# Places for gathered rows lent by tables and weights, and a longer count, in a graph-network kernel

## The chip, the cores and the metric

The kernel runs on one core of one Trainium2 chip. The metric is the device time of one execution in microseconds (us), and the time of a kernel is the median over its runs. The engines are PE (TensorE, matmul; its loading of weights is shown apart as PEld), DVE (VectorE), ACT (ScalarE), POOL (GpSimd) and SP (SyncE, which issues DMAs).

## What is computed

A graph layer over N = 12,500 nodes of D = 256 features and M = 212,500 edges (src, dst), which come sorted by dst, followed by a mixture of 64 experts with the best two per node, a normalization over the nodes, and a layer normalization with a residual:

```python
deg_out = jnp.clip(jax.ops.segment_sum(ones, src, num_segments=n), 1.0)
deg_in = jnp.clip(jax.ops.segment_sum(ones, dst, num_segments=n), 1.0)
h = feats * jax.lax.rsqrt(deg_out)[:, None]
m = jax.ops.segment_sum(h[src], dst, num_segments=n) * jax.lax.rsqrt(deg_in)[:, None]
gc = m @ W_gc + b_gc
x = gc + (feats @ W_res + b_res)
y = x + _moe_ff(x, Wg, bg, w1, b1, w2, b2)      # top 2 of E = 64 experts, H = 512
y = (y - mean(y, 0)) * rsqrt(var(y, 0) + eps) * gamma + beta
return _layernorm(feats + y)
```

The change touches the first third: the gathering of h[src], its sums by dst, and the counting of deg_out.

## The kernel before, in words

**Rows.** The edges are cut into rows of 128. There are 1,593 of them, and a count CA = 480 of them makes the first phase. For a row c, Pool issues one indirect DMA that gathers 128 lines of 1 KB (128 KB) by `src_col[:, c]` into a place of 128 x 256 numbers in SBUF. DVE makes a one-hot matrix from the row's dst (`one_hot`, L881 to L895), 12 rows ahead (`AHEAD`); there are 5 tiles of four. PE multiplies one-hot by place into a PSUM bank (L924); in the trace one row is two matmul records. Twelve rows make a group (GR): then ACT copies the bank (`out_of`, L959), PE turns the sums (`turn`, L974), and DVE adds them to the nodes' sums in `acc` (`to_nodes`, L997). All of this is written out in order by `go` (L1691 to L1707): each row's gather, its matmul, the one-hot of the row 12 behind it, and then all other work whose row number has come (`at_row`, `later`, a heap of row numbers). So every engine has one fixed order, and a step is placed by a row number.

**What a row reads.** Rows below NE = 104 gather from the input x itself, since the scaled features h do not exist yet; the factor of each edge's source goes into the one-hot (`look` L606 on PE and `found` L614 on DVE look it up). Meanwhile x is loaded into `xs` (a part of `acc`), scaled by ACT and DVE (`scaled`, L625 and L627) and written by SP to h_d in DRAM (`h_out`, L631). Rows from 104 on gather from h_d.

**Where a row waits.** Rows 0 to 39 (EA) go to parts of `xs` that are still free, rows 40 to 47 to eight pieces of a table (`flat`, in the tile `tables`); both are issued ahead of the loop (`first_row` L461, `wait_at` L456). From row 48 (ES) on, rows go to a ring of RINGS x RR = 5 x 4 = 20 places. The first gather of each four waits for the last matmul of the four that had the places before (`row_last`, by `sync`).

**What else SP brings.** Around row 22 `zero_piece` (L670) copies zeros into two pieces of `acc` that the groups' sums are added to, and again at row 104 into four more. `lines_in` at row 92 clears a tail of two tables on DVE (L661) and loads lines of dst and src. `src_in` at row 98 loads src once more for counting, `weights_in` at row 106 loads the tables of weights (`wcat`, `bias`, and so on) that the phase behind row 480 needs.

**Counting.** deg_out has to be compared with what the kernel assumed. 68 groups (KG) of 25 columns of src are split into digits (`digits`), turned into one-hots by DVE (`compare`, `compare_b`, both through `hot`, L248) and ACT (Sign, L1590), and counted by PE in two PSUM banks (`tally`, L1595 and L1599). The numbers that DVE compares with, `lane_p`, lie in the upper part of the first of these banks. The groups stand evenly between the rows COUNT_FROM = 112 and COUNT_TO = 426. Five steps behind them (`counted` to `counted_e`, at COUNT_TO + 12 + 3 i) end in `bad_n`, a single number (L1627), which every engine reads behind row 480 to choose a branch (L1715). Beside counting, DVE marks (rows 108 to 158) and squeezes (rows 160 to about 353) the repeated edges, and lays them out in new columns behind that.

**Behind row 480.** The other rows go on in the same way, now with the node part of the layer in between, then the experts follow, and the normalizations.

Of the kernel before, what the change touches and what calls it, by code (L numbers as in the profile page):

```python
# [8 lines left out]
F32 = mybir.dt.float32  # L9
F16 = mybir.dt.float16  # L10
BF16 = mybir.dt.bfloat16
# [10 lines left out]
D = 256  # L22
# [10 lines left out]
EP = 125  # L33
EC = M // EP
# [12 lines left out]
HC = HG * GR  # L47
# [12 lines left out]
CA = PA * GR  # L60
# [5 lines left out]

NE = 104
EA = 40
ES = 48
ET = 56  # L70
NOWHERE = 2 * NP
BEHIND = (1 << 14) - 1
# [78 lines left out]
def gnn_moe_kernel(  # L151
# [18 lines left out]
    V, S, T, GP = nc.vector, nc.scalar, nc.tensor, nc.gpsimd  # L170
# [38 lines left out]
    slot_a = route.tile([P, NSLOT], I32)  # L209
# [9 lines left out]
    flat = tables.rearrange("p a b c -> p (a b c)")  # L219
# [10 lines left out]
    bias = edge.tile([P, DL], F32)  # L230
# [194 lines left out]
    def x_in(t0, n):  # L425
        r = rows(t0)
        nc.sync.dma_start(xs[:r, t0 : t0 + n], part_of(x, t0, n))
# [25 lines left out]
    place = place[:, :EC]  # L453


    def wait_at(c):  # L456
        if c < EA:
            return xs[:, ET + c]
        return flat.bitcast(F32)[:, (c - EA) * D : (c - EA + 1) * D]

    def first_row(c):  # L461
        GP.indirect_dma_start(
            out=wait_at(c),
            out_offset=None,
            in_=x,
            in_offset=bass.IndirectOffsetOnAxis(ap=src_col[:, c : c + 1], axis=0),
        )
# [52 lines left out]

    for v in range(OH):
        compare_lo(v)
    for c in range(EA, ES):
        first_row(c)
    V.tensor_copy(top_i, top8)
    V.tensor_scalar(
# [105 lines left out]


    def check_order():
        junk = flat.bitcast(BF16)[:EP, : EC - 1]
        V.tensor_tensor(junk, dst_t[:, 1:], dst_t[:, : EC - 1], op=ALU.is_lt)
        V.tensor_scalar(
            junk, junk, 0.5, None, op0=ALU.is_gt, op1=ALU.add, accum_out=bad[:EP, 6:7]
        )
# [9 lines left out]
        )  # L649

    def check_windows():
        junk = flat.bitcast(F32)[:, :HC]
        for k, (lim_of, op) in enumerate(((0.0, ALU.is_lt), (float(W), ALU.is_ge))):
            V.tensor_scalar(
                junk, rel[:, :HC], lim_of, None,
                op0=op, op1=ALU.add, accum_out=bad[:, k : k + 1],
            )

    def lines_in():
        V.tensor_mul(root, d_in, r_in)  # L660
        V.memset(l_dst[:, LAST:], BEHIND)  # L661
        V.memset(l_src[:, LAST:], 0)
        for t, e in ((l_dst, dst), (l_src, src)):
            nc.sync.dma_start(
                t[: NL - 1], e[HE : HE + (NL - 1) * L].rearrange("(p c) -> p c", c=L)
            )
            nc.sync.dma_start(t[NL - 1 :, :LAST], e[M - LAST :].rearrange("(p c) -> p c", p=1))
# [169 lines left out]
    def at_row(c, f):  # L837
        heapq.heappush(todo, (c, len(given_at), f))
        given_at.append(c)
# [16 lines left out]
    def sync(i, on):  # L856
        tc.add_manual_dep(
            i.ins, on.ins.name,
            mybir.DependencyInfo(mybir.DependencyClass.Sync, mybir.DependencyReason.DATA),
            reason="one wait for several",  # L860
        )
# [36 lines left out]
    def row(c):  # L898
        g, j = divmod(c, GR)
        last = j == GR - 1 or c == ROWS - 1  # L900
        u, k = divmod(c, RR)
        if c < ES:
            h_row = wait_at(c)
        else:
            r = ring[u % RINGS]
            h_row = r[:, k]
            i = GP.indirect_dma_start(  # L907
                out=r[:, k, :D],
                out_offset=None,
                in_=x if c < NE else h_d,  # L910
                in_offset=bass.IndirectOffsetOnAxis(ap=src_col[:, c : c + 1], axis=0),
            )
            if k == 0 and u - RINGS in row_last:
                sync(i, row_last.pop(u - RINGS))
        n = D
        if g >= HG:
            n = D1
            if k == 0:
                S.copy(r[:, :, D], mark[:, c - HC : c - HC + RR])
        if j == 0:  # L920
            p_of[g] = p_banks[g % 2][:, :D1]
            own(g)
        v, m = divmod(c, OR)
        i = T.matmul(  # L924
            p_of[g][:, :n], o_of[v][:, m], h_row[:, :n], start=j == 0, stop=last
        )
        if m == 0:
            sync(i, o_last.pop(v))
        if m == OR - 1:
            del o_of[v]  # L930
        if k == RR - 1 and c >= ES:
            row_last[u] = i
        if last:
            later(c, lambda t: out_of(g, n, t), 0.5)

# [708 lines left out]
        at_row(5 * i + 2, lambda t, a=t0 + n - BY_DVE: scaled(a, BY_DVE, False))  # L1644
        at_row(5 * i + 5, lambda t, t0=t0, n=n: h_out(t0, n))
    for i, (t0, n) in enumerate(second):
        at_row(min(t0 + n - ET, ES) + 1, lambda t, t0=t0, n=n: x_in(t0, n))
        a = 28 + 9 * i
        for k in range(n):
            at_row(a + k, lambda t, a=t0 + k: scaled(a, 1, True))  # L1650
        at_row(a + n, lambda t, t0=t0, n=n: h_out(t0, n))
# [4 lines left out]
        at_row(max(0, 4 * u - 35), lambda t, u=u: compare_lo(u))  # L1656
    for i in (0, NPW // 2):
        at_row(22, lambda t, i=i: zero_piece(i))
    for i, f in enumerate((check_order, check_runs, check_windows)):
        at_row(60 + 10 * i, lambda t, f=f: f())  # L1660
    at_row(92, lambda t: lines_in())
    at_row(98, lambda t: src_in())
    for i in (1, NPW // 2 + 1, 2, NPW // 2 + 2):
        at_row(104, lambda t, i=i: zero_piece(i))
    at_row(106, lambda t: weights_in())
    at_row(NE, lambda t: lanes())
    COUNT_FROM, COUNT_TO = 112, CA - 54
    for k in range(KG):
        c = COUNT_FROM + (COUNT_TO - COUNT_FROM) * k // KG
        if k % CK == 0:  # L1670
# [604 lines left out]
```

## Time and profile before

| | |
|---|---|
| three runs | 2998.6, 2994.85, 2983.08 us; median 2994.85 us |
| the profiled execution | 3004.58 us, of which its span is 3002.8 us |
| mean granted clock of PE | 0.94 |
| busy, share of the span | PE 82%, PEld 62%, DVE 55%, ACT 26%, POOL 68% |
| DMA | 563.72 MB, mean 188 GB/s |

All times below are in microseconds from the start of the span unless said otherwise. A line of a timeline gives the start, the duration, the engine, the source line, the operation, what is written from what is read, the count, and in brackets how long the engine was idle before it and what ended that. A line "A <- B: t, n, m" of the waits says that A waited t us in all for B, in n places, the longest m us. A line of windows gives the stretch, its length, then busy time and instructions for each engine that is asked for, the granted clock, the share of the DMA engines and GB/s. L followed by a number is a line of the kernel.

### The profile page before, as it was taken

The numbers are of one execution on the slowest core, as the hardware profiler recorded it, in microseconds if no ns is written. First come the engines' busy times: TensorE is split into PE (matmuls) and PEld (weight loads), VectorE is DVE, ScalarE is ACT, GpSimd is POOL, SyncE is SP. The second block draws the span as 40 slices with busy tenths as digits, with TensorE's granted clock in tenths as the row PEclk, the third lists the DMA queues.
The fourth block names the chain that finished last, engine by engine and source line by source line (L and its number), as shares of the span: only waits on it lengthen the run. The fifth ranks groups of instructions, "written<-read, shape, count | busy, mean of one in ns | idle before, by whom it ended". The sixth has DMA issues, their size and how long they took to land. (4 is left out here: it accounts for less than half of the span.)

```text
span 3002.8 us, 43600 instructions
## 1 busy us (share of the span) xinstructions
PE 2469.6 (82%) x13517; PEld 1865.1 (62%) x13517; DVE 1664.2 (55%) x6230; ACT 783.7 (26%) x2250; POOL 2048.3 (68%) x2145
## 2 busy tenths in 40 slices
PE   4756666777888777798999998999995799899895
PEld 4634445545655444576777777666773577777795
DVE  8868887644788634465344433343454544444247
ACT  2723444421111000122222222222221122222346
POOL 7677777677777777777777777777772767775200
PEclk9988989998999998999999999999997899999998
DMA  6953333336555444556666676676884567777868
GB/s 208 351 182 98 101 98 100 97 111 216 174 148 143 135 124 123 167 172 184 180 192 197 200 209 203 203 227 204 258 240 135 169 211 234 256 245 245 279 204 283
DMA packets 287463, 563.72 MB, mean 188 GB/s; under 512 B 56518, under 2 KB 194294, under 8 KB 279030
## 3 DMA queue, kind: packets, MB, share of 16 engines
q0 software_dynamic: 99120, 268.99, 30.9%
q1 hardware_dynamic: 174310, 278.75, 29.2%
q10 hardware_dynamic: 13792, 13.10, 1.4%
q8 instruction: 110, 1.80, 0.2%
q14 instruction: 131, 1.07, 0.1%
HBM read 494.32 MB, written 66.34 MB: 187 GB/s over the span
## 5 line engine op out<-in xcount | busy, mean ns | idle before, releaser
L907 POOL DMA_INDIRECT ring<-h_d,src_col x1489 | 1461.3, 981 | 469.3 <-issue 400.5
L924 PE MATMUL p<-ring,o 128*128 128x257 f32 (+1 forms) x3090 | 994.1, 422 | 217.2 <-DMA ring<-h_d,src_col 151.4
L924 PEld LDWEIGHTS p<-ring,o 128*128 128x128 f32 x3090 | 538.0, 202 | 410.2 <-DMA ring<-h_d,src_col 208.0
L894 DVE TENSOR_SCALAR o<-lane,rel 128x128 f32<-128x128 f32 x1489 | 380.2, 298 | 271.8 <-PE p L924 270.8
L1419 ACT ACTIVATE acc<-p,acc 128x128 f32<-128x128 f32 (+8 forms) x360 | 137.3, 381 | 742.6 <-PE p L1408 424.9
L1443 DVE TENSOR_TENSOR acc<-yp_a,acc 128x256 f32<-128x256 f32 (+7 forms) x127 | 53.2, 419 | 431.1 <-PE yp_a L1436 431.1
L1408 PE MATMUL p<-acc 128*128 128x128 f32 (+8 forms) x1440 | 248.5, 295 | 8.0 <-ACT s L959 2.1
L1408 PEld LDWEIGHTS p<-acc 128*128 128x128 f32 x1440 | 220.5, 191 | 53.7 <-ACT acc L1419 33.8
L1436 PE MATMUL yp_a<-acc 128*128 128x256 f32 (+7 forms) x1016 | 250.4, 391 | 0.0
L1922 PE MATMUL yp<-w,h 128*128 128x256 f32 (+7 forms) x1032 | 239.6, 382 | 7.3 <-DVE yo L1927 7.3
L1895 PE MATMUL hp<-xT,w 128*128 128x112 f32 (+17 forms) x1056 | 214.5, 358 | 31.2 <-DVE xT L1886 29.2
L248 DVE TENSOR_TENSOR acc<-bank,acc 125x2450 bf16<-125x2450 bf16 (+1 forms) x136 | 185.1, 1361 | 87.7 <-PE bank L1595 74.7
L1590 ACT ACTIVATE acc<-lane_b,acc 125x128 bf16<-125x128 bf16 x544 | 168.5, 389 | 232.8 <-PE bank L1599 226.0
L1895 PEld LDWEIGHTS hp<-xT,w 128*128 128x128 f32 x1056 | 178.1, 203 | 64.3 <-DVE xT L1886 33.4
L1595 PE MATMUL bank<-acc 125*128 125x98 bf16 x1156 | 104.3, 219 | 133.4 <-DVE acc L248 116.0
L1899 ACT ACTIVATE h<-hp,w 128x128 f32<-128x128 f32 (+16 forms) x264 | 113.0, 430 | 376.3 <-PE hp L1895 345.8
L1595 PEld LDWEIGHTS <-acc 125*128 125x128 bf16 x1156 | 84.7, 104 | 201.3 <-issue 158.0
L1922 PEld LDWEIGHTS yp<-w,h 128*128 128x128 f32 (+7 forms) x1032 | 167.9, 170 | 56.5 <-DVE yo L1927 10.2
L1436 PEld LDWEIGHTS yp_a<-acc 128*128 128x128 f32 (+7 forms) x1016 | 171.5, 174 | 48.4 <-issue 5.8
L1933 POOL DMA_INDIRECT z_d<-yo,tables x129 | 125.1, 970 | 92.1 <-DVE gate L1909 41.0
L1867 POOL DMA_INDIRECT xg<-xb_d,tables x129 | 125.3, 971 | 51.4 <-PE xtp L1882 18.5
L1372 POOL DMA_INDIRECT acc<-xa_d,tables x127 | 123.4, 972 | 42.8 <-issue 31.4
(375 smaller groups left out, 3481.8 us busy)
## 6 DMA issues: line engine op xcount, KB each, us to landing
w<-in_wpack SPq DMA_DIRECT2D x64, 1026.0 KB
acc<-in_wpack SPq DMA_DIRECT2D x128, 512.0 KB
ring<-h_d,src_col POOLq DMA_INDIRECT x1489
tables<-h_d SPq DMA_DIRECT2D x99, 128.0 KB
acc<-acc_d SPq DMA_DIRECT2D x14, 896.0 KB
xt<-in_x ACTq DMA_DIRECT2D x48, 256.0 KB
zt<-z_d SPq DMA_DIRECT2D x24, 512.0 KB
z<-in_x SPq DMA_DIRECT2D x12, 1024.0 KB
```

What stands on the lines that cost most here:

```text
L248: V.tensor_tensor(o.rearrange("p k (a b) -> p k a b", b=2), lane_b[:p, None, :n] .rearrange("p k (a b) -> p k a b", b=2) .to_broadcast([p, ...
L894: o_last[u] = V.tensor_scalar(o_of[u][:, j], lane, rel[:, c : c + 1], None, op0=ALU.is_equal)
L907: i = GP.indirect_dma_start(out=r[:, k, :D], out_offset=None, in_=x if c < NE else h_d, in_offset=bass.IndirectOffsetOnAxis(ap=src_col[:, ...
L924: i = T.matmul(p_of[g][:, :n], o_of[v][:, m], h_row[:, :n], start=j == 0, stop=last)
L1408: T.matmul(hp, w1[:, c, j * P : (j + 1) * P], xT[:, c, :m], start=c == 0, stop=c == 1,)
L1419: S.activation(h1[:, j, :m], hp_of.pop((q, j)), AF.Gelu, bias=b1_a[i % 2][:, j : j + 1])
L1436: T.matmul(y, h1[:, j, k * P : k * P + n], w2[:, j], start=j == 0, stop=j == 3)
L1590: S.activation(s_los[k % 2][:, j], lane_b[:EP], AF.Sign, bias=nbs[u % 2][:, i, j : j + 1])
L1595: T.matmul(deg, o_los[k % 2][:, j], o_his[k % 2][:, j], start=k + j == 0, stop=False)
L1867: GP.indirect_dma_start(out=g, out_offset=None, in_=of, in_offset=bass.IndirectOffsetOnAxis(ap=at[:, k : k + 1], axis=0),)
L1895: T.matmul(hp[:, :m], w1[:, c, j * P : (j + 1) * P], xT[:, c, :m], start=c == 0, stop=c == 1,)
L1922: T.matmul(yp[:r], h1[:, j, k * P : k * P + r], w2[:, j], start=j == 0, stop=j == 3,)
```

## The change

**Places.** `wait_at` becomes `place_of`, which serves all rows. Behind the first 40 rows there are 16 lent places (EX): eight in `flat` as before, five in `wcat`, two in `slot_a`, one in `bias`. These tiles get their own contents only later (`weights_in` and behind it). Rows 40 to 55 go to the lent places and are issued ahead of the loop, rows 56 to 75 to the ring's 20, rows 76 to 91 to the lent places once more, and from row 92 on the ring alone goes round. A gather into a ring place waits for the last matmul of the four rows that had it before, now counted by turns of the ring (`turn_of`); a gather into a lent place waits for the matmul that read it.

**What makes room.** The three checks of the edges (rows 60, 70, 80) wrote scratch into `flat`; they now write it into `ends` and `raw`, and the first two have changed places. `lines_in` moves from row 92 to row 93. The last two loads of x come at the row of EA instead of ES.

**The count.** It stands between rows 108 and 454 instead of 112 and 426, and its five last steps move with it, to rows 466 to 478.

```diff
 NE = 104
 EA = 40
-ES = 48
+EX = 16
...
-    def wait_at(c):
+    lent_rows = [flat.bitcast(F32)[:, k * D : (k + 1) * D] for k in range(8)]
+    by_w = wcat.rearrange("p a d -> p (a d)")
+    lent_rows += [by_w[:, k * D : (k + 1) * D] for k in range(5)]
+    lent_rows += [slot_a.bitcast(F32)[:, k * D : (k + 1) * D] for k in range(2)]
+    lent_rows += [bias[:, :D]]
+
+    def place_of(c):
         if c < EA:
-            return xs[:, ET + c]
-        return flat.bitcast(F32)[:, (c - EA) * D : (c - EA + 1) * D]
+            return xs[:, ET + c], None
+        turn_of = EX + RINGS * RR
+        k = (c - EA) % turn_of if c < EA + turn_of + EX else c - EA - turn_of
+        if k < EX:
+            return lent_rows[k], None
+        u, k = divmod(k - EX, RR)
+        return ring[u % RINGS][:, k], u % RINGS
...
-    for c in range(EA, ES):
+    for c in range(EA, EA + EX):
         first_row(c)
...
     def check_order():
-        junk = flat.bitcast(BF16)[:EP, : EC - 1]
+        junk = ends[:, : EC - 1]
...
     def check_windows():
-        junk = flat.bitcast(F32)[:, :HC]
+        junk = raw[:, 2 * EC + EC // 2 : 2 * EC + EC // 2 + HC]
...
-        if c < ES:
-            h_row = wait_at(c)
-        else:
-            r = ring[u % RINGS]
-            h_row = r[:, k]
+        h_row, turn_of = place_of(c)
+        if c >= EA + EX:
             i = GP.indirect_dma_start(
...
-            if k == 0 and u - RINGS in row_last:
-                sync(i, row_last.pop(u - RINGS))
+            if k == 0 and turn_of in row_last:
+                sync(i, row_last.pop(turn_of))
...
-        if k == RR - 1 and c >= ES:
-            row_last[u] = i
+        if k == RR - 1 and turn_of is not None:
+            row_last[turn_of] = i
...
-        at_row(min(t0 + n - ET, ES) + 1, lambda t, t0=t0, n=n: x_in(t0, n))
+        at_row(min(t0 + n - ET, EA) + 1, lambda t, t0=t0, n=n: x_in(t0, n))
...
-    for i, f in enumerate((check_order, check_runs, check_windows)):
+    for i, f in enumerate((check_runs, check_order, check_windows)):
         at_row(60 + 10 * i, lambda t, f=f: f())
-    at_row(92, lambda t: lines_in())
+    at_row(EA + 2 * EX + RINGS * RR + 1, lambda t: lines_in())
...
-    COUNT_FROM, COUNT_TO = 112, CA - 54
+    COUNT_FROM, COUNT_TO = 108, CA - 26
```

The order of Pool shows the places. Before, from the end of its preparations: first the 48 rows ahead of the loop, then the ring, with 56 gathers from x (rows 48 to 103) and 376 from h_d (rows 104 to 479).

```order
L449 IOTA rel 125x1716
L462 DMA acc<-in_x,src_col 128x256 x40
L462 DMA tables<-in_x,src_col 128x256 x8
L907 DMA ring<-in_x,src_col 128x256 x56
L907 DMA ring<-h_d,src_col 128x256 x376
```

Now 56 rows stand ahead of the loop, then come the ring, the lent places again, and the ring.

```order
L475 DMA acc<-in_x,src_col 128x256 x40
L475 DMA tables<-in_x,src_col 128x256 x8
L475 DMA wcat<-in_x,src_col 128x256 x5
L475 DMA slot_a<-in_x,src_col 128x256 x2
L475 DMA bias<-in_x,src_col 128x256
L917 DMA ring<-in_x,src_col 128x256 x20
L917 DMA tables<-in_x,src_col 128x256 x8
L917 DMA wcat<-in_x,src_col 128x256 x5
L917 DMA slot_a<-in_x,src_col 128x256 x2
L917 DMA bias<-in_x,src_col 128x256
L917 DMA ring<-in_x,src_col 128x256 x12
L917 DMA ring<-h_d,src_col 128x256 x376
```

The number of gathers and their sequence by rows are the same; only where they land differs, and eight more are issued ahead of the loop.

The second place is PE's order at the end of the count. Before, from the last tally on (`bank_123<-acc`), one record is one row's matmul (p_124, p_125), tab is a step of the weights' tables, q the turning of a group's sums, and the last line is the sum of `bad`:

```order
L1599 MATMUL bank_123<-acc 128x98
L924 MATMUL p_125<-ring,o 128x257
L924 MATMUL p_124<-ring,o 128x257 x7
L1491 MATMUL tab<-acc 128x64 x2
L924 MATMUL p_124<-ring,o 128x257 x3
L1610 MATMUL bank_122<-acc,steps 128x98
L924 MATMUL p_124<-ring,o 128x257 x2
L924 MATMUL p_125<-ring,o 128x257 x4
L1624 MATMUL bank_123<-bad,ones_f 1x1
```

Behind it come 32 more rows before PE reads `bad_n`. Now:

```order
L1609 MATMUL bank_123<-acc 128x98
L934 MATMUL p_124<-ring,o 128x257 x2
L984 MATMUL q<-ident,s 128x128 x2
L934 MATMUL p_124<-ring,o 128x257 x8
L934 MATMUL p_125<-ring,o 128x257 x2
L1620 MATMUL bank_122<-acc,steps 128x98
L934 MATMUL p_125<-ring,o 128x257 x2
L984 MATMUL q<-ident,s 128x128 x2
L934 MATMUL p_125<-ring,o 128x257 x4
L1634 MATMUL bank_123<-bad,ones_f 1x1
L934 MATMUL p_125<-ring,o 128x257 x4
L984 MATMUL q<-ident,s 128x128 x6
```

The sum of `bad` now stands four rows ahead of the end of the first phase, and the read of `bad_n` follows the last line. On DVE and ACT the count's steps move in the same way, and the sequence on SP is the same.

More of the change, by code (lines that the diff above doesn't have):

```diff
@@ L453, in gnn_moe_kernel @@
     place = place[:, :EC]
-    def wait_at(c):
-        if c < EA:
-            return xs[:, ET + c]
-        return flat.bitcast(F32)[:, (c - EA) * D : (c - EA + 1) * D]
+    lent_rows = [flat.bitcast(F32)[:, k * D : (k + 1) * D] for k in range(8)]
[3 more added lines that the diff above has]
+    lent_rows += [bias[:, :D]]
+    assert len(lent_rows) == EX and EX % RR == 0
+    def place_of(c):
+        if c < EA:
+            return xs[:, ET + c], None
[5 more added lines that the diff above has]
+        return ring[u % RINGS][:, k], u % RINGS
     def first_row(c):
         GP.indirect_dma_start(
-            out=wait_at(c),
+            out=place_of(c)[0][:, :D],
             out_offset=None,
@@ L901, in row @@
         u, k = divmod(c, RR)
-        if c < ES:
-            h_row = wait_at(c)
-        else:
-            r = ring[u % RINGS]
-            h_row = r[:, k]
+        h_row, turn_of = place_of(c)
+        if c >= EA + EX:
             i = GP.indirect_dma_start(
-                out=r[:, k, :D],
+                out=h_row[:, :D],
                 out_offset=None,
@@ L918, in row @@
             if k == 0:
-                S.copy(r[:, :, D], mark[:, c - HC : c - HC + RR])
+                S.copy(ring[turn_of][:, :, D], mark[:, c - HC : c - HC + RR])
         if j == 0:
```

## The prediction

> **What bounds the kernel now.** I read the page's costliest groups first, then Pool's pace in a quiet stretch, then Pool's waits, then Pool's timeline around the longest one. In the groups, the numbers behind the bar are busy time, mean of one and idle time before; a row of edges is one Pool issue and two matmul records.
>
> ```profile
> L907 POOL DMA_INDIRECT ring<-h_d,src_col x1489 | 1461.3, 981 | 469.3 <-issue 400.5
> L924 PE MATMUL p<-ring,o 128*128 128x257 f32 (+1 forms) x3090 | 994.1, 422 | 217.2 <-DMA ring<-h_d,src_col 151.4
> ```
>
> Pool's row gathers cost 1461.3 + 469.3 us, most of the idle part being "issue", time that waits for nothing. PE's idle time before rows is spent waiting for the gathers. The next row is 100 us behind the stretch that the change touches: busy time and instructions of PE, PEld, DVE, ACT and Pool, the clock, DMA share, GB/s.
>
> ```profile
> 700.00:800.00 100.00, 85.13 (x364) 59.40 (x364) 67.90 (x348) 16.52 (x53) 75.94 (x79) 0.95 0.59 177
> ```
>
> Pool issues 79 rows in 100 us, 1.266 us each, though it is "busy" for only 76%: 0.95 us of work and 0.30 us between two. The 1,593 rows are a chain on Pool, and a microsecond is won where Pool waits for something else, provided that PE follows. So I look at what Pool waits for (total, times, longest) and where the longest one is.
>
> ```profile
> POOL ring L907 <- issue: 414.2, 1345, 3.1
> POOL ring L907 <- PE p L924: 34.3, 58, 11.9
> ```
>
> ```profile
> 102.79 0.95 POOL L907 DMA_INDIRECT ring<-in_x,src_col  x1 [0.30 <-issue]
> 115.62 0.95 POOL L907 DMA_INDIRECT ring<-in_x,src_col  x1 [11.88 <-PE p L924]
> ```
>
> The ring holds 20 rows and begins at row 48, so this is row 68 waiting for the matmuls of rows 48 to 51. Why PE is late stands on SP, DVE and PE:
>
> ```profile
> 90.64 5.32 SPq L670 DMA_DIRECT2D acc<-acc_d  x2
> 109.04 0.42 DVE L997 TENSOR_TENSOR acc<-q,acc 128x256 f32 x1 [11.81 <-ACT acc L625]
> 111.59 1.14 PE L606 MATMUL bank<-rel,lines 128*128 128x98 bf16 x12 [4.51 <-DVE rel L614]
> 113.94 1.84 PE L924 MATMUL p<-ring,o 128*128 128x256 f32 x6
> ```
>
> DVE adds its first sums into a piece of acc that SP's two zeroing DMAs, issued at 90.6 to 96.0, have to clear (ACT, which the row names, had long been done). For 11.8 us DVE makes no one-hots, PE runs dry, and Pool behind it.
>
> The second place shows when rows are counted on PE (two matmuls a row, first block) and on Pool (second block). An instruction that crosses an edge counts twice, so read them to one row.
>
> ```profile
> 0.00:188.00 188.00, 76.62 (x240) 42.26 (x240) 0.94 0.84 279
> 188.00:310.00 122.00, 61.62 (x154) 28.50 (x154) 0.83 0.33 95
> 310.00:430.00 120.00, 63.26 (x174) 29.15 (x174) 0.91 0.35 101
> 430.00:608.00 178.00, 93.95 (x260) 43.60 (x261) 0.91 0.34 98
> ```
>
> ```profile
> 0.00:188.00 188.00, 77.01 (x75) 0.94 0.84 279
> 188.00:310.00 122.00, 95.17 (x89) 0.83 0.33 95
> 310.00:430.00 120.00, 90.87 (x91) 0.91 0.35 101
> 430.00:608.00 178.00, 125.27 (x130) 0.91 0.34 98
> ```
>
> At 188 us PE has done 120 rows and Pool has issued 48 + 75 = 123: a lead of 3. It grows by 12 and by 4, to 19, and in the last stretch both do 130: the ring is full and PE sets the pace, 178 / 130 = 1.369 us a row. Pool's rows in two stretches say what it lost:
>
> ```profile
> L907 POOL DMA_INDIRECT ring<-h_d,src_col x179 | 186.8, 1044 | 56.3 <-issue 47.5 <-PE bank L1599 2.7 <-PE p L924 2.3
> L907 POOL DMA_INDIRECT ring<-h_d,src_col x130 | 126.3, 972 | 54.7 <-issue 38.0 <-PE p L924 6.5 <-PE bank L1595 5.4
> ```
>
> From 188 to 430 us idle time is 56.3 against 179 x 0.30 = 53.7: no wait worth the name. From 420 to 600 it is 54.7 against 130 x 0.30 = 39.0: 15.7 us of waiting. That is all there is to win in the second place.
>
> **The change, part by part.** *36 places behind row 40.* Row 68 no longer waits; its place is the thirteenth of the ring's, empty since the start. Row 76 is the first to reuse one: it waits for row 40's matmul. Pool would be there at 115.6 - 11.6 + 8 x 1.266 = 114 us, when PE is past row 50 (the x6 at 113.94 are behind it). Each of rows 76 to 91 has such a wait on the row 36 before it, with at least ten rows to spare at PE's pace above. At row 92 the ring's 20 places alone go round again, so the look-ahead shrinks to 20 at row 112. The term is 11.88 - 0.30 = 11.6 us off Pool's path, if nothing is late next. Next is row 104, the first to read h_d:
>
> ```profile
> 123.47 15.53 SPq L631 DMA_DIRECT2D h_d<-acc  x6
> 161.29 0.95 POOL L907 DMA_INDIRECT ring<-in_x,src_col  x1 [0.30 <-DMA ring<-in_x,src_col]
> 162.85 0.95 POOL L907 DMA_INDIRECT ring<-h_d,src_col  x1 [0.61 <-issue]
> ```
>
> ```profile
> DMA  9998999999999988864386731575104760009971
> ```
>
> Row 104 will be issued at 162.85 - 11.6 = 151.3 us. The last h_d writes are issued by 139.0, and in the second answer (busy tenths of the DMA engines in 140 to 150 us, 0.25 us a digit) the load falls at 144 and is gone by 147. But Pool now sends 11.6 / 1.266 = 9 more gathers of 128 KB into a stretch that is full:
>
> ```profile
> 110.00:120.00 10.00, 8.41 (x70) 7.15 (x70) 9.57 (x51) 7.38 (x17) 3.47 (x4) 0.77 1.09 383
> 180.00:190.00 10.00, 7.41 (x44) 4.37 (x43) 5.84 (x13) 0.92 (x3) 7.87 (x8) 1.00 0.32 90
> ```
>
> 1.2 MB at 383 GB/s is 3.1 us, if they share with SP's transfers: the writes are done at 147 to 150, still ahead of 151.3. If they did not share it would be 0; I take 3 us of delay on SP and 0 to 1.5 us on Pool. The Trainium skill, "DMA: Bandwidth & Descriptors", section "Issuing engines are not separate DMA queues", says that all issuers' DMAs run on the same 16 engines and interleave. It speaks against the change and for the 3.1 us; the load near 390 GB/s at either pace of Pool agrees with it.
>
> The same fullness lets DVE gain less than Pool. SP's next flood (lines, src, four zero pieces, weights; over by 180 us, in the second row above) starts when DVE has cleared the tail of the lines:
>
> ```profile
> 147.68 0.47 DVE L661 MEMSET lines<- 99x500 int32 x1
> ```
>
> DVE is busy 9.57 us of 10 in the row of 110 us and at 95% up to here, so it cannot be here 11.6 us earlier; marking and counting wait for that flood. Against that, in before they began some 10 us after their data could be had, since rows came late. I take 8 us of the 11.6 for PE and DVE, between 0 and 11.6; the other 3.6 us come out of the ring's lead, not out of Pool's time.
>
> *Counting at rows 108 to 454.* 68 groups stand every 346 / 68 = 5.09 rows, no longer every 314 / 68 = 4.62. Between rows 120 and 430 there were 68 - 8 / 4.62 = 66.3, and now (430 - 120) / 5.09 = 60.9: 5.4 fewer. What is one worth to PE? DVE's two compares and PE's tallies take turns (waits in 500 to 600 us, then one group on DVE):
>
> ```profile
> PE bank L1595 <- DVE acc L248: 27.3, 31, 1.5
> DVE acc L248 <- PE bank L1595: 25.4, 23, 3.4
> ```
>
> ```profile
> 544.23 1.43 DVE L248 TENSOR_TENSOR acc<-bank,acc 125x2450 bf16<-125x2450 bf16 x1 [1.15 <-PE bank L1599]
> 546.87 1.29 DVE L248 TENSOR_TENSOR acc<-bank,acc 125x2176 bf16<-125x2176 bf16 x1 [0.39 <-PE bank L1595]
> 627.71 3.71 PE L924 MATMUL p<-ring,o 128*128 128x257 f32 x16
> ```
>
> At least the two compares, 1.43 + 1.29 = 2.7 us. At most what a group adds to free rows: PE does 8 rows in 3.71 us (last row, behind the counting), 0.46 us each, and 4.62 rows of the full-ring stretch take 4.62 x 1.369 = 6.3 us, so 6.3 - 2.1 = 4.2 us. 5.4 groups are 15 to 23 us off PE's path. The 3.6 us of lead spent above come back off: 11 to 19 us against 15.7 us of waits. Pool gains 11 to 15.7; I take 13. The Trainium skill, "PSUM — Partial Sum Buffer", section "PSUM bank collisions raise a hardware error", says to guard PSUM by bank and not by address. The compares read lane_p in the bank where the tallies add, so by it they must take turns, as the two wait rows show; guarded by address, compares would hide beside tallies, spreading would win little, and the sum would stay near the first term.
>
> *The end of the count beside the branch.* Pool reads bad_n before row 480. Its last input now comes behind row 475's matmuls, no longer around row 447:
>
> ```profile
> 636.19 0.14 DVE L1627 TENSOR_SCALAR bad_n<-bank 1x1 int32<-1x1 f32 x1
> 671.48 0.94 POOL L907 DMA_INDIRECT ring<-h_d,src_col  x1 [0.30 <-PE p L924]
> 687.16 5.83 PE L924 MATMUL p<-ring,o 128*128 128x257 f32 x16 [10.78 <-ACT ring L919]
> ```
>
> Today bad_n is 35 us early for row 480 (second row). With Pool n rows ahead when PE ends the last tallies near row 459, Pool is at row 480 after (21 - n) x 1.266 us, and bad_n is ready after 16 x 0.46 us and about 1 us of DVE: a wait from n = 14 on, 7 us at n = 20. I expect n near 11 and a cost of 0 to 3 us, 0.5 taken. Queued behind are row 480 on Pool and, on PE, DVE and ACT, the second phase's start; PE stands there 10.8 us already for ACT's first load, 13 rows behind Pool, which leaves seven places.
>
> The rest costs nothing: the three checks' scratch moves and two of them swap (same sizes, same engine); clearing the lines at row 93 waits for row 83's matmul, and the one-hots ahead of it on DVE wait for row 87's already; the last two x loads go one or two rows earlier.
>
> **Sum.** -11.6 - 13 + 1 (row 104) + 0.5 (branch) = -23 us on the profiled execution, 3004.58 to 2981.5. That one stands 9.7 us above the median of the three runs, so for the median 2994.85 - 23 = **2972 us**.
>
> **Rivals.** *Spreading wins nothing* (PE's pace has another cause, its clock of 0.91 for one): the ring fills again, Pool gains only the 8 us that PE gained at the start: 2987. For it: the clock in those windows. Against: the two rows of mutual waits. *PE and DVE start no earlier* (the flood is at the same time as now): the lead is 12 rows at row 120, the ring fills, and Pool ends where PE does, 15 to 23 us earlier by the missing groups, less some of it behind row 430: about -16, 2979. For it: full DMA up to 144 us. *Slower*: the branch takes over. If PE is still 20 rows behind at row 459 and goes on at 1.369 us a row, the wait before row 480 is 16 x 1.369 + 1 - 1.266 = 21.6 us with only the 8 us won: 2994.85 + 13.6 = 3008. It needs the ring full to the end, and begins to count from n = 14; against it speaks that PE has nothing but rows to do behind row 459. That the order is not what the diff says can be left out: Pool's order shows the 36 places.
>
> **How the numbers follow.** Forecast 0.69, nothing by spreading 0.10, no earlier start 0.15, the branch 0.04, more than all known waits 0.02. The bounds of the terms give -27 to -16 for the forecast; the three runs spread by 8 us around it. With the first two rivals 2959 to 2988. About 15 us, 0.5%, is what a measurement can tell from no change here: faster 0.76 (the forecast but for its edge, and most of "no earlier start"), same 0.20, slower 0.04.
>
> **What would show it.** Right: no Pool gap over 2 us at rows 68 to 104; row 104 issued near 151 us; a lead under 18 rows at row 300 and hardly any "PE" waits on Pool from there to 460; row 480 issued 22 to 26 us earlier than 671.5 and the rest shifted as a whole. Wrong: a gap at row 104 or at 112; a full ring at row 300 again; a gap of several us before row 480.

## The result and the profile after

The changed kernel takes 2973.67 us (median of 7 runs, 2963.15 to 2980.56), the kernel before 2993.52 us (7 runs). The ratio is 0.994, with a 95% interval of 0.9918 to 0.9961: 20 us less. 2972 us were forecast, 23 us less than the median of the three runs that the forecast started from.

The profiled executions differ by 24.0 us of span (3002.8 to 2978.8). Where that comes from is read on Pool, since its gathers are the chain. First the group of all gathers of the changed kernel, then Pool's waits from the start to 720 us (total, times, longest):

```profile
L917 POOL DMA_INDIRECT ring<-h_d,src_col x1489 | 1458.1, 979 | 458.5 <-issue 402.0
```

```profile
POOL ring L917 <- issue: 126.2, 405, 2.2
POOL ring L917 <- PE bank L1609: 4.6, 15, 0.3
POOL ring L917 <- PE p L934: 4.0, 13, 0.3
POOL ring L917 <- PE bank L1605: 2.7, 9, 0.3
POOL ring L917 <- PE q L984: 2.4, 3, 1.8
```

"PE p" was 23.0 us in 21 places up to there, with a longest wait of 11.9 us; now it is 4.0 us in 13 places of 0.3 us each. That is Pool's ordinary gap of 0.30 us, with PE's name on it only because a semaphore of PE's came last in it. Pool no longer waits for PE anywhere up to row 480. What is left are three other waits. Pool's timeline shows the gathers of rows 68, 76, 104, 113 and 480:

```profile
104.01 0.95 POOL L917 DMA_INDIRECT ring<-in_x,src_col  x1 [0.30 <-PE yp_a L527]
114.02 0.97 POOL L917 DMA_INDIRECT tables<-in_x,src_col  x1 [0.30 <-PE tab L527]
151.44 0.94 POOL L917 DMA_INDIRECT ring<-h_d,src_col  x1 [1.81 <-PE q L984]
164.62 1.00 POOL L917 DMA_INDIRECT ring<-h_d,src_col  x1 [2.24 <-issue]
650.94 0.94 POOL L917 DMA_INDIRECT ring<-h_d,src_col  x1 [1.22 <-issue]
```

Row 68 goes 11.6 us earlier than before, row 480 20.5 us earlier. Three waits are new or longer: 1.5 us at row 104 (0.3 before), 1.9 us at row 113, 0.9 us at row 480, each without the gap of 0.30 us. The two stretches behind the second term, here 180 to 420 us (the prediction took 188 to 430 us) and 420 to 600 us:

```profile
L917 POOL DMA_INDIRECT ring<-h_d,src_col x176 | 187.3, 1064 | 53.6 <-issue 48.7 <-PE bank L1609 2.4 <-PE bank L1605 1.2
L917 POOL DMA_INDIRECT ring<-h_d,src_col x143 | 138.3, 967 | 43.6 <-issue 39.0 <-PE bank L1609 1.8 <-PE bank L1605 1.2
```

From 420 to 600 us Pool issues 143 rows where it issued 130; its idle time is 43.6 us against 143 x 0.30 = 42.9. The full ring is gone.

DVE's first add, DVE's last step of the count, and PE's wait at the start of the second phase:

```profile
108.81 0.42 DVE L1007 TENSOR_TENSOR acc<-q,acc 128x256 f32 x1 [11.59 <-DMA acc<-acc_d]
647.48 0.15 DVE L1637 TENSOR_SCALAR bad_n<-bank 1x1 int32<-1x1 f32 x1 [5.03 <-PE bank L1634]
666.06 5.21 PE L934 MATMUL p<-ring,o 128*128 128x257 f32 x16 [10.70 <-ACT ring L929]
```

DVE still waits for the zeroing DMAs, nearly as long as before (11.59 and 11.81 us). So the change took away nothing of what makes PE late at row 68. It took away that Pool has to wait for it. How far Pool is ahead of PE, the copies of two groups' sums on ACT tell (rows 299 and 419, before and after):

```profile
457.94 0.35 ACT L959 COPY s<-p 128x256 f32<-128x256 f32 x1
623.27 0.38 ACT L959 COPY s<-p 128x257 f32<-128x257 f32 x1
```

```profile
429.85 0.35 ACT L969 COPY s<-p 128x256 f32<-128x256 f32 x1
586.59 0.38 ACT L969 COPY s<-p 128x257 f32<-128x257 f32 x1
```

PE ends row 299 28 us earlier and row 419 37 us earlier. Counting Pool's gathers up to these times, Pool was 20 and 22 rows ahead before, and is 7 and 10 rows ahead now.

From row 480 on the pace did not change: 79 rows in 100 us, as before.

```profile
700.00:800.00 100.00, 83.87 (x368) 57.37 (x366) 76.44 (x402) 15.74 (x55) 76.11 (x79) 0.95 0.61 182
```

The shift of 20.5 us at row 480 is the median's 20 us. It is 21.6 us at row 1400. Most of the rest of the 24.0 us lies behind that row, where the issues of the one profile were some 4 us shorter in all; the medians don't show that.

### The profile page after: what moved, and what is told of

Read it like the earlier page. It is cut to its first block, busy times and chain, and to the rows that moved or that the text cites. A ratio compares the mean times of both kernels' runs of the same rounds, so it can differ in the third digit from the quotient of the medians.

```text
span 2978.8 us, 43601 instructions
## 1 busy us (share of the span) xinstructions
PE 2456.0 (82%) x13517; PEld 1858.0 (62%) x13517; DVE 1663.0 (56%) x6230; ACT 783.8 (26%) x2250; POOL 2043.7 (69%) x2145
## 5 line engine op out<-in xcount | busy, mean ns | idle before, releaser
L934 PE MATMUL p<-ring,o 128*128 128x257 f32 (+1 forms) x3042 | 974.9, 420 | 208.5 <-DMA ring<-h_d,src_col 154.8
L934 PEld LDWEIGHTS p<-ring,o 128*128 128x128 f32 x3042 | 523.7, 200 | 394.2 <-DMA ring<-h_d,src_col 208.8
L248 DVE TENSOR_TENSOR acc<-bank,acc 125x2450 bf16<-125x2450 bf16 (+1 forms) x136 | 185.1, 1361 | 81.5 <-PE bank L1605 79.9
```

The costliest lines, as they stand in the source:

```text
L248: V.tensor_tensor(o.rearrange("p k (a b) -> p k a b", b=2), lane_b[:p, None, :n] .rearrange("p k (a b) -> p k a b", b=2) .to_broadcast([p, ...
L934: i = T.matmul(p_of[g][:, :n], o_of[v][:, m], h_row[:, :n], start=j == 0, stop=last)
```

## The experiments

In each, the number to look at is when Pool issues row 480: 671.5 us in before, 650.9 us in the changed kernel. Each was timed beside the kernel before on its own chip, so ratios compare, and times only nearly.

| kernel | wait at row 68 | row 480 | against before | median us | ratio (95%) |
|---|---|---|---|---|---|
| changed kernel | none | 650.9 | -20.5 | 2973.67 | 0.994 (0.9918 to 0.9961) |
| places only | none | 664.4 | -7.1 | 2987.99 | 0.9979 (0.9963 to 0.9996) |
| count only | 11.3 | 659.7 | -11.8 | 2983.71 | 0.9971 (0.9957 to 0.9985) |
| numbers in their own bank | 11.8 | 666.2 | -5.3 | 2989.06 | 0.9989 (0.9973 to 1.0005) |
| memsets | 4.2 | 656.0 | -15.5 | 2981.73 | 0.996 (0.9946 to 0.9975) |
| changed, memsets | none | 653.3 | -18.1 | 2973.09 | 0.9927 (0.991 to 0.9944) |
| memsets, count | 6.6 | 651.6 | -19.9 | 2977.27 | 0.9944 (0.993 to 0.9958) |
| changed, late end | none | 660.5 | -10.9 | 2979.15 | 0.995 (0.9937 to 0.9963) |
| changed, no count | none | 647.5 | -24.0 | 2973.53 | 0.9935 (0.9922 to 0.9948) |

The last four ran first on another chip, on which the kernel before took 3817.51 us; these runs stand at the end of this section.

### Places only

```diff
-    COUNT_FROM, COUNT_TO = 108, CA - 26
+    COUNT_FROM, COUNT_TO = 112, CA - 54
```

> The 36 places, with the count back at rows 112 to 426. My theory: two gains that add up, the places bringing Pool only what PE gains at the start. Row 68 does not wait, row 104 is issued near 151 us, but PE still spends about 6.3 us on a group of the count, so that the ring is full again at rows 300 to 412 and Pool waits there 11 to 16 us for PE; row 480 is issued at 660 to 664 us in place of 671.5, and the time is 8 to 11 us below before (ratio 0.9965). Rival 1, the places do it all (PE's earlier start is what keeps the ring from filling): no waits from row 300 on, row 480 at 651, ratio 0.993. Rival 2, all that Pool wins early is given back at the full ring: row 480 at 671, ratio 1.000.

Row 104 goes at 151.35 us, and the ring is full again. Pool from 420 to 600 us:

```profile
L917 POOL DMA_INDIRECT ring<-h_d,src_col x129 | 124.1, 962 | 56.6 <-issue 37.3 <-PE bank L1609 7.2 <-PE bank L1605 6.6
```

129 rows (130 before), 56.6 us of idle time where 129 gaps make 38.7: 18 us of waits. Row 480 comes 7.1 us earlier, just short of what was expected, since PE is ahead by 4 to 8 us at rows 119 to 155 and by 6.9 us at row 419. The ratio, 0.9979, stands for 6 us in place of 8 to 11. Rivals 1 and 2 fall. What Pool wins at row 68 beyond PE's own win is spent on a fuller ring.

### Count only

```diff
-    COUNT_FROM, COUNT_TO = 112, CA - 54
+    COUNT_FROM, COUNT_TO = 108, CA - 26
```

> The kernel before with nothing changed but the count at rows 108 to 454. My theory: row 68 waits 11.9 us as before; the groups stand 5.09 rows apart, PE gets ahead, and the waits of 14 to 15.7 us at rows 300 to 412 are gone: row 480 at 656 to 658 us, ratio 0.995. Rival, PE's pace between rows 300 and 412 has another cause than the groups (its clock): Pool waits there as before, row 480 at 669 to 672, ratio 1.000.

The row of Pool's wait at row 68, then of 420 to 600 us:

```profile
115.30 0.95 POOL L907 DMA_INDIRECT ring<-in_x,src_col  x1 [11.56 <-PE p L924]
```

```profile
L907 POOL DMA_INDIRECT ring<-h_d,src_col x143 | 138.4, 968 | 43.6 <-issue 38.4 <-PE bank L1599 2.4 <-PE bank L1595 1.5
```

The first wait is untouched, the second gone, with 143 rows as in the changed kernel. The 15.1 us of waits between rows 275 and 425 went; some came back, among others 1.2 us at row 104, 0.8 us at row 480 and 1.6 us in longer issues between rows 104 and 300, so that 11.8 us stay, a little less than expected. The rival, PE's clock, does not explain it: from 188 to 310 us and from 310 to 430 us the clock was 0.78 and 0.90 here and 0.83 and 0.91 in before, and PE ended row 299 15.4 us earlier all the same (442.56 us, 457.94 before). From 430 to 600 us it was 0.94 against 0.91, so a part of the waits there may have gone by the clock; how large it is was not separated. The two parts add up: 7.1 + 11.8 = 18.9 us against 20.5 us together.

### The compares' numbers in a PSUM bank of their own

```diff
-    lane_p = banks[0][:, 7 * E :].bitcast(BF16)
+    lane_p = yp_a.rearrange("p a d -> p (a d)")[:, 7 * E :].bitcast(BF16)
```

> The kernel before, with the count where it was, and the numbers that DVE compares with (lane_p) moved out of the PSUM bank in which the tallies add, into the bank of yp_a, which nothing else uses between rows 104 and 480. My theory, turns by bank: compares and tallies no longer wait for each other (27 and 25 us of mutual waits between 500 and 600 us go down to under 5 each), a group costs PE near 4.5 us in place of 6.3, and Pool's waits at rows 300 to 412 go without any spreading: row 480 at 656 to 658, ratio 0.995. Rival, the group is slow by its own work or by the clock: waits on Pool stay at 11 to 16 us, row 480 at 669 to 672, ratio 1.000.

The waits from 500 to 600 us that name the compares (L248), the tallies or the rows (L924) first, then Pool from 420 to 600 us and from 160 to 310 us:

```profile
DVE acc L248 <- PE bank L1599: 26.8, 15, 3.4
PE p L924 <- DMA ring<-h_d,src_col: 20.2, 48, 1.6
```

```profile
L907 POOL DMA_INDIRECT ring<-h_d,src_col x141 | 137.7, 976 | 43.0 <-issue 38.7 <-PE bank L1599 3.0 <-DMA ring<-h_d,src_col 0.3
```

```profile
L907 POOL DMA_INDIRECT ring<-h_d,src_col x100 | 115.8, 1158 | 31.3 <-issue 26.8 <-PE bank L1599 1.5 <-DMA acc<-in_src 1.2
```

"PE bank L1595 <- DVE acc L248", 27.3 us before, is gone. DVE's waits for the tallies, which were expected under 5 us, stay (26.8 us); by the order of the code DVE now is a group ahead and waits for its buffers. PE waits for gathers, and Pool's full ring is gone, with the count still at rows 112 to 426: PE is 6 and 8 rows behind Pool at rows 299 and 419. The clock was higher as well (0.86, 0.96 and 0.96 from 188 to 310, 310 to 430 and 430 to 600 us; 0.83, 0.91 and 0.91 before). But the memsets of the next experiment had 0.86, 0.93 and 0.95, and their ring stayed full. So the turns at the bank set most of PE's pace, and the rival does not hold alone. The gain at row 480 is 5.3 us in place of 13 to 15, and the ratio's interval takes in no change. The third block says where it went: the issues of 160 to 310 us took 1158 ns in the mean, in before

```profile
L907 POOL DMA_INDIRECT ring<-h_d,src_col x107 | 115.7, 1082 | 33.0 <-issue 29.0 <-PE bank L1599 0.9 <-DMA ring<-h_d,src_col 0.9
```

1082 ns. From row 104 to 300 the part of the issues above 0.95 us is 27.8 us, 19.3 in before and 20.9 with the count alone; the 6.9 us between this run and the count alone are about what the two gains differ by (11.8 and 5.3 us). Why the issues were longest here was not settled; the last section says what they wait for.

### Two memsets in place of the first zeroing DMAs

```diff
-        at_row(22, lambda t, i=i: zero_piece(i))
+        at_row(22, lambda t, i=i: V.memset(piece(i), 0.0))
```

> The kernel before, with the first two zeroed pieces of acc cleared by DVE at row 22 (two memsets of 128x1792) in place of two DMAs. My theory, PE is late at row 68 because DVE waits 11.8 us for those DMAs: the memsets cost DVE 2 to 4 us, the first add comes near 101 us in place of 109.0, Pool waits at row 68 about 4 us in place of 11.9, and since PE sets the pace at the full ring, its 8 us reach row 480: 663 to 664 us, ratio 0.997. Rival, DVE is late for its own work and the wait only covers it: the first add comes at 107 to 110, row 68 waits 10 to 12 us, ratio 1.000. Rival 2, Pool wins 8 us at row 68 and gives them back at the full ring: row 480 at 671.

DVE's two memsets, its first add, and Pool's row 68:

```profile
87.50 1.55 DVE L1658 MEMSET acc<- 128x1792 f32 x1 [0.32 <-issue]
89.44 1.55 DVE L1658 MEMSET acc<- 128x1792 f32 x1 [0.38 <-issue]
...
102.50 0.42 DVE L997 TENSOR_TENSOR acc<-q,acc 128x256 f32 x1 [0.23 <-issue]
```

```profile
109.53 0.94 POOL L907 DMA_INDIRECT ring<-in_x,src_col  x1 [4.52 <-PE p L924]
```

The first add comes at 102.5 us without a wait, row 68 waits 4.2 us: the cause of PE's lateness is shown, and both rivals fall. The gain is twice what was expected, 15.5 us at row 480. PE is ahead by 6.4 us at row 107, by 10.8 us at row 299 and by 15.4 us at row 419. The last 4.6 us come between rows 347 and 395, where the clock was higher. PE's busy time, clock, DMA share and GB/s from 430 to 600 us, in before, with the places only, and here:

```profile
430.00:600.00 170.00, 118.46 (x977) 0.91 0.34 97
```

```profile
430.00:600.00 170.00, 121.17 (x962) 0.88 0.33 97
```

```profile
430.00:600.00 170.00, 116.01 (x1000) 0.95 0.36 103
```

A record of PE took 121, 126 and 116 ns in the mean, at a clock of 0.91, 0.88 and 0.95. While the ring is full, PE sets the pace, so the higher clock would account for these 4.6 us: with the count where it was, Pool waited 5.0 us between rows 300 and 425, 15.3 us in before and 17.5 us with the places only. What made the clock differ between these kernels was not tried.

### The changed kernel with the memsets

The edit is that of the experiment above, made in the changed kernel.

> The changed kernel, with the first two pieces cleared by two DVE memsets at row 22 in place of two DMAs. My theory, Pool's chain: at row 68 nothing waits any more, so the 6 to 9 us that DVE and PE win do not reach Pool; what does is the missing 1.8 MB of DMA, by which the last writes of h_d land some 4 us earlier, so that the waits at row 104 (1.5 us) and row 113 (1.9 us, for the gather of row 105) shrink: row 480 at 647.5 to 651 in place of 650.9, time 0 to 3.5 us under the changed kernel (2970 to 2974, ratio to before 0.993). Rival, PE's lead still counts somewhere behind row 120: 6 to 9 us more, row 480 at 642 to 645, 2965.

> The changed kernel with two DVE memsets at row 22 in place of the first two zeroing DMAs, on another chip than the one that took 3817 us for before. My theory, Pool's chain: row 68 waits for nothing, so what DVE and PE win at the start (6 to 9 us) does not reach Pool; only the waits at rows 104 and 113 (1.5 and 1.9 us) shrink, since 1.8 MB of DMA are gone: row 480 at 647.5 to 651 us against 650.9, time 2970 to 2974, ratio to before 0.992 to 0.994. Rival, PE's lead still counts behind row 120: row 480 at 642 to 645, 2965.

Nothing is won at row 480: 653.3 us, 2.4 us later than in the changed kernel and later than the 647.5 to 651 us expected. The ratio to before is 0.9927 (0.991 to 0.9944), in whose interval the changed kernel's 0.994 lies, so the times tell no difference of a few us. The same memsets that brought 12 us in the kernel before bring none here that these runs can tell, since Pool had no wait left for PE that they could shorten. The waits around rows 104 to 113 went from 3.4 us to 2.3 us (0.9 us at row 107, 1.3 us at row 113); 3.4 us were lost to longer issues between rows 56 and 300. The rival falls.

### The memsets and the longer count, with 20 places

Both edits above, in the kernel before.

> The kernel before with its 20 places, the two memsets and the count at rows 108 to 454: whether 36 places are needed once the cause of the wait at row 68 is smaller. My theory, the waits add up: 4.2 us of waiting are left at row 68, the full ring is gone as with the count alone: row 480 at 671.5 - 7 - 12 = 652 to 655 us, time 16 to 19 us below before (2975 to 2978, ratio 0.994). Rival, the memset's 15 us and the count's 12 us are the same microseconds at the full ring and do not add: row 480 at 656 to 659, ratio 0.996.

> The kernel before with its 20 places, the two memsets and the count at rows 108 to 454. My theory, the waits add up: 4.2 us are left at row 68 and the full ring is gone: row 480 at 652 to 655 us, time 16 to 19 us below before (ratio 0.994). Rival, the 15 us of the memsets and the 12 us of the count are the same microseconds at the full ring: row 480 at 656 to 659, ratio 0.996.

Row 480 at 651.6 us, 19.9 us earlier, at the edge of the 652 to 655 us expected. Row 68 waits 6.6 us, more than the 4.2 us of the memsets alone, and the full ring is gone. So the two waits add up, as the theory has it. The two gains do not: 15.5 and 11.8 us make 27.3 us, 7.4 us more than both bring together, so in that part the rival was right, though not in its time. Two lines in place of the 36 places reach the changed kernel's time, as far as these runs can tell (0.9944 and 0.994).

### The count ending at row 474

```diff
-    COUNT_FROM, COUNT_TO = 108, CA - 26
+    COUNT_FROM, COUNT_TO = 108, CA - 6
```

> The changed kernel with the count ending at row 474 in place of 454, so that its last five steps come behind row 479. My theory, the branch: Pool is at row 480 at 650 us as in the changed kernel, two or three rows ahead of PE, bad_n is ready only when PE has done row 479 and the five steps with their changes of engine are through, 3 to 6 us behind Pool: row 480 at 653 to 656 in place of 650.9, and the time 2 to 5 us over the changed kernel (2976 to 2979). Rival 1, the last steps hide (Pool waits under 1.5 us): row 480 at 650 to 651. Rival 2, spreading further still helps PE and so Pool: row 480 under 649.

> The changed kernel with the count ending at row 474 in place of 454. My theory, the branch: bad_n is ready only when PE has done row 479 and the five last steps are through, 3 to 6 us behind Pool: row 480 at 653 to 656 us in place of 650.9, time 2 to 5 us over the changed kernel (2976 to 2979, ratio to before 0.995). On the other chip the wait before row 480 was some 23 us with PE 16 to 20 rows behind; here PE is 2 to 10 rows behind. Rival 1, the steps hide: row 480 at 650 to 651. Rival 2, spreading further still helps: under 649.

PE's last row and the two matmuls of the count's last steps, DVE's last step, and Pool's first gather behind the branch:

```profile
653.08 1.23 PE L934 MATMUL p<-ring,o 128*128 128x257 f32 x2 [1.55 <-DMA ring<-h_d,src_col]
...
654.53 0.59 PE L1620 MATMUL bank<-acc,steps 128*128 128x98 f32 x2
...
656.85 0.19 PE L1634 MATMUL bank<-bad,ones_f 128*1 128x1 f32 x2 [1.30 <-DVE bad L1629]
```

```profile
657.07 0.15 DVE L1637 TENSOR_SCALAR bad_n<-bank 1x1 int32<-1x1 f32 x1 [0.28 <-PE bank L1634]
```

```profile
660.53 0.94 POOL L917 DMA_INDIRECT ring<-h_d,src_col  x1 [10.32 <-DVE o L907]
```

The branch it is, but it costs 10.0 us and not 3 to 6. bad_n is ready at 657.2 us, 7 us behind Pool's end of row 479 (650.2 us), a little over what the theory gave; what it lacked are the 3.3 us from there to Pool's first gather. They are the same in every run in which Pool waits for bad_n: in the changed kernel 647.63 to 650.94, here 657.22 to 660.53, on the other chip 838.2 to 841.5. Pool's queue shows what it does in them; first the load of the number, then a step at the line of the branch:

```profile
L1725 POOLq TENSOR_LOAD <-bad_n x1: 491/491/491, 657.3 to 657.3; - x1
L1726 POOLq INC_SWDGE_SEM x1: 1289/1289/1289, 658.3 to 658.3; - x1
```

So it is the time in which the number is read (0.49 us) and the branch taken, with 1.29 us for that one step. So the 0.9 us in the changed kernel aren't a late bad_n (it was ready 2.4 us before Pool was) but this reading.

### The changed kernel without the count

```diff
-    for k in range(KG):
-        c = COUNT_FROM + (COUNT_TO - COUNT_FROM) * k // KG
...
-    for i, f in enumerate((counted, counted_b, counted_c, counted_d, counted_e)):
+    for i, f in enumerate((counted_c, counted_d, counted_e)):
...
-        V.tensor_scalar_max(d_out, deg, 1.0)
...
+        V.memset(d_out, 1.0)
+        V.memset(bad[:, 5:6], 0.0)
```

> The changed kernel with the count of deg_out left out (no digits, compares, Sign, tallies; the check of the degrees is taken as passed, so the check of edges that it stands for is not made). My theory, spread over 346 rows the count is hidden but for its marks on Pool's issues: the lengthened issues beside compares (5 to 6 us in rows 112 to 480) and part of the branch's wait go, row 480 at 643 to 650, time 0 to 8 us under the changed kernel (2966 to 2974). Rival 1, the count still bounds Pool somewhere: more than 12 us. Rival 2, the lengthened issues come from marking and squeezing and grow when DVE does these faster: row 480 at 651 or later.

> The changed kernel with the count of deg_out left out (and the check of the degrees that it serves). My theory, spread over 346 rows the count is hidden but for its marks on Pool's issues: row 480 at 643 to 650 us, time 0 to 8 us under the changed kernel (2966 to 2974, ratio 0.991 to 0.994). Rival 1, the count still bounds Pool somewhere: row 480 under 639. Rival 2, the lengthened issues come from marking and squeezing and grow when DVE does these faster: row 480 at 651 or later.

Row 480 at 647.5 us, 3.4 us earlier than in the changed kernel; the median, 2973.53 us, is that of the changed kernel. All 68 groups together, spread over 346 rows, cost at most these 3.4 us. They are not the issues beside compares, as expected: Pool from 160 to 310 us, in the changed kernel and here,

```profile
L917 POOL DMA_INDIRECT ring<-h_d,src_col x104 | 116.6, 1121 | 33.6 <-issue 30.0 <-PE bank L1609 1.5 <-PE bank L1605 0.9
```

```profile
L917 POOL DMA_INDIRECT ring<-h_d,src_col x106 | 118.2, 1116 | 32.3 <-issue 29.5 <-PE p L934 2.4 <-DMA ring<-h_d,src_col 0.3
```

has issues of 1121 and 1116 ns. The lengthening belongs to other work of DVE, marking and squeezing above all, which are in both (the last section shows it); rival 2 was right in that, though not in its time. Most of the 3.4 us are the waits at rows 113 and 480, 2.8 us, which went.

### The same four on a slower chip

| kernel | median us | ratio to before there (95%) |
|---|---|---|
| changed, memsets | 3815.16 | 0.9996 (0.9976 to 1.0017) |
| memsets, count | 3820.61 | 1.0007 (0.9986 to 1.0028) |
| changed, late end | 3808.37 | 0.9983 (0.9959 to 1.0007) |
| changed, no count | 3739.67 | 0.9803 (0.9771 to 0.9835) |

On that chip the engines stood still where nothing of the program held them. A row of DVE from the kernel with the late end, then Pool's waits from 500 to 700 us:

```profile
109.21 0.30 DVE L587 COPY n_b<-q 128x133 f32<-128x133 f32 x1 [43.87 <-remote]
```

```profile
POOL ring L917 <- PE p L934: 34.9, 11, 6.4
```

In the first three Pool was 16 to 24 rows ahead of PE almost throughout, so the ring was full, and neither places nor spreading helped; only leaving the count out did (2%). With the late end, Pool waited 23 us for bad_n. What slowed that chip is open. The changed kernel itself did not run there, but the one that differs from it by the memsets was no faster than before. The gain needs a PE that follows.

## Why the prediction was right, point by point

**The bound.** That Pool's chain of gathers is the path, and that a microsecond is won only where Pool waits, holds best where it is tested hardest: the memsets win 12 us in the kernel before and none that can be told in the changed kernel, on the same DVE wait. By its own signs the prediction was not right throughout: row 480 comes 20.5 us earlier, not 22 to 26, and there is a gap at row 104 (1.5 us) and one of 1.9 us next to row 112.

**Row 68, -11.6 us.** As forecast: row 68 at 104.01 us, row 76 at 114.02 us (114 forecast), row 104 at 151.44 us (151.3 forecast).

**Row 104 and the DMAs, +1 us.** The mechanism was right and the size too small. SP's last six writes of h_d run to 143.2 us where they ran to 139.0:

```profile
127.26 15.94 SPq L644 DMA_DIRECT2D h_d<-acc  x6
```

They are 4.2 us late; the working had 3.1 us by sharing. Row 104 waited 1.5 us, the upper end. With 1.8 MB less (the memsets in the changed kernel) these writes run to 136.2 us, and row 104 does not wait. The Trainium skill, "DMA: Bandwidth & Descriptors", section "Issuing engines are not separate DMA queues", says that DMAs of all issuers interleave on the same engines, and the trace agrees. Not seen was row 113: DVE clears the tail of the lines at 147.6 us as it did before, so SP's next flood starts when it did, but Pool's first gathers from h_d now fall into it. Row 105's gather landed 10.2 us behind its issue (8.0 before), at 162.9 us, and row 113's gather, whose only wait in the trace is for the semaphore of row 105's, was issued at 164.6 us after 1.9 us of waiting. What takes the 1.7 us between the two is open. The waits at rows 104 and 113 make 3.1 us more than before, not 1.

**PE starts 8 us earlier.** PE was 4 to 11 us ahead at rows 119 to 155. SP's flood came as late as the rival "PE and DVE start no earlier" wanted (the clearing ahead of it at 147.6 us, 147.68 before); PE was ahead all the same.

**Spreading, -13 us of 15.7.** The waits went whole: 15.1 us between rows 275 and 425 to nothing. The lead of 7 to 10 rows shows that PE has room to spare, more than the lead under 18 that was forecast. The rival "spreading wins nothing" falls with the count alone (11.8 us). But the clock that it named counts beside the spacing: from 430 to 600 us it was 0.95, 0.91 before, and with the memsets alone, at 0.95 and the old spacing, only 5.0 us of waits were left. How the 15.1 us divide between spacing and clock is open. The Trainium skill, "PSUM — Partial Sum Buffer", section "PSUM bank collisions raise a hardware error", which says to guard by bank, was the reason to believe in the turns of compares and tallies; with the numbers in a bank of their own PE's waits for the compares were gone. That shows that this kernel guards by bank, and what it costs here, not what the chip does without a guard.

**What the sum left out.** Pool's issues between rows 104 and 300 took 3.3 us longer in all than before (22.6 us above 0.95 us each, 19.3 before). The prediction had no term for it. The parts as measured make -11.6 - 15.1 + 3.1 + 3.3 + 0.9 = -19.4 us against the -20.5 us at row 480; the rest is in shorter issues ahead of row 104. The forecast's -23 us had 2.1 us too little for rows 104 and 113, nothing for the longer issues, and 0.4 us too little for the branch, and left 2.1 us of the full ring's waits standing that went. That these partly cancel is luck, and it brings the forecast closer than its terms were.

**The branch, +0.5 us.** 0.9 us measured, at a lead of 2 to 4 rows and not near 11, so for another reason: the 3.3 us of reading the number and branching, which the working had at nothing. The rival on the slower side was real as a mechanism: with the count's end 20 rows later, at the same lead, it cost 10.0 us, half of the gain at row 480.

## What to carry to other kernels

Cost a wait at the engine that sets the end, and not where it is longest: shortening the same wait of DVE was worth 12 us of time in one kernel and nothing that could be told in the other, which differ in how far the chain may run ahead and in how evenly the count stands. When more buffers remove a wait, look at once for the next place where the same buffers fill; here only a third of the gain (7.1 of 20.5 us) would have been left without thinning out the work that slows the consumer. Before buying buffers, look for what makes the consumer late: two memsets and the thinner count reached the same time with the 20 places that were there.

## What the runs showed of the hardware

**Pool's issues stretch beside some DVE work.** An issue of 0.95 us took 4.37 us in the kernel before, beside a scan on DVE:

```profile
211.74 4.37 POOL L907 DMA_INDIRECT ring<-h_d,src_col  x1 [0.30 <-issue]
```

```profile
211.58 3.53 DVE L785 TENSOR_TENSOR_SCAN lines<-lines 99x1624 f32<-99x1624 bf16 x1
```

Over rows 104 to 300 this is 17 to 28 us in the ten kernels, more than any single term here. Leaving out the count changed it by 1.7 us. The traces tell which work it is. In before, 46 of the 376 issues of rows 104 to 479 took more than 1.05 us, and each ended 0.8 to 1.06 us behind the end of a DVE instruction, about the time of an issue alone, as if it had begun only then; the issue above ends 1.0 us behind the scan. Of the short issues some 30% end so, by chance. 103 issues started within a compare of the count (L248) that had 0.3 us or more to go, and none of them was held to its end; of 37 that started so within marking or squeezing (L746 to L823), 27 were. The Trainium skill, "SBUF — State Buffer", section "Who interferes with whom", says that some DVE instructions take a port pair that GpSimd shares, and that the other then waits for the whole instruction; these rows agree. What sets the compares apart was not tried.

**A PE with fewer matmuls was granted less, and it did not matter.** Without the count, PE ran 192 records from 188 to 310 us in place of 614, its clock there fell from 0.85 to 0.59, and one matmul record of the rows took 0.53 us in place of 0.39. Pool, not PE, set the pace, and nothing was lost. The rows' matmuls in the changed kernel and without the count:

```profile
188.00:310.00 122.00, 66.06 (x171) 0.85 0.32 93
```

```profile
188.00:310.00 122.00, 93.22 (x176) 0.59 0.32 94
```

**Reading one number to branch cost 3.3 us** from the end of the instruction that wrote it to Pool's next gather, on both chips, wherever Pool waited for it. Where the number was 35 us old, in before, Pool's gather had only its usual 0.30 us of idle time.
